# Layer 1's attention of a two-layer gated block: two items per turn, with the products of quarter size of both in one row and all others after them

## The chip, the cores and the metric

The kernel runs on one core of one Trainium2 chip. The metric is the device time of one execution in microseconds (us): the median of 13 runs. The engines are called as in the profile: PE (matrix products; PEld is its load of the stationary operand), DVE (vector), ACT (scalar functions), POOL, and SP, which issues DMAs. All five run side by side, each in its own order, and wait for each other by semaphores. All data of the stage in question are fp32, and PE takes two passes for one fp32 product, so that a product is two MATMUL records in the profile.

## The reference

Two layers, each a cross attention and a feed-forward part, both added to `x` through a gate. Batch 32, 112 rows of 256 in a batch, 375 context rows of 128. Layer 0's feed-forward is a recurrence over the batch, layer 1's a mixture of 64 experts with 8 chosen per token. What is changed is layer 1's attention:

```python
# B, N, M = 32, 112, 375; 16 heads of 64
qh = (q @ Wq).reshape(B, N, 16, 64).transpose(0, 2, 1, 3)     # q = layernorm(x), 256 wide
kh = (kv @ Wk).reshape(B, M, 16, 64).transpose(0, 2, 1, 3)    # kv = ctx, 128 wide
vh = (kv @ Wv).reshape(B, M, 16, 64).transpose(0, 2, 1, 3)
attn = softmax(einsum('bhnd,bhmd->bhnm', qh, kh) / 8)
out = einsum('bhnm,bhmd->bhnd', attn, vh).transpose(0, 2, 1, 3).reshape(B, N, 1024)
x = x + tanh(g_xattn[1]) * (out @ Wo + bo)
```

## The kernel before

The kernel has four stages in a row: layer 0's attention, the recurrence, layer 1's attention (about 810 to 1980 us of the profiled span), and the mixture of experts with its sums. Only the third is touched.

Its unit is an **item**: one batch element `b` and a group `g` of four heads, so 128 items, `n = 4b + g`. Per item these steps run; the letters are used in the rest of the text.

- **K0, K1** (`keys1`, line 796): the keys of two heads each, one product 128x128 by 375 columns; ACT copies the result to SBUF (line 800).
- **V0, V2** (`values1`, line 811): the values, two and one products of 256 columns; ACT copies the first (line 818), DVE the second (line 816).
- **S** (`scores1`, line 835): the scores of four heads, eight products of 64 rows and 64 or 48 columns of the array, four of which fit into the array at once. DVE takes the negative maximum (line 839), ACT the exponential with its sum (line 840).
- **N** (`normal1`, lines 850 and 852): DVE divides the four heads by their sums.
- **T0, T1, T2** (`turn1`, line 864): the transposes of a third of the 375 columns each, four heads in one PSUM tile; DVE copies T0 (line 871), ACT T1 and T2 (line 869).
- **A** (`values_of`, line 889): attention times values, 24 products of 64 (or 61) rows and 64 columns of the array, four at once, into two PSUM tiles, the even and the odd half of the contraction; DVE copies one and adds the other (lines 896 and 897).
- **O** (`output1`, line 907): two of the eight chunks of the output product of the batch element; after the fourth item DVE adds the bias, the gated sum and the row statistics (lines 912, 185, 156, 157), and the batch element's **route** begins.

S and A use the array in quarters of 64x64; all other products use it whole or with 112 to 128 rows. `queries1` (Q, line 783) makes one of eight chunks of the queries of two later batch elements per item, `turned1` turns the normalised rows.

`route(b)` is a generator for the choice of experts. Each `next` runs it to its next `yield`; the loop calls it twice per item, and 18 calls finish it, so that two or three are under way at any time. Three of its calls use PE: the fourth (transposes, line 225), the sixth (`pu`, lines 233 and 235) and the eighth (`pos`, lines 260 to 265). The tile `pos` is written in the eighth call and read for the last time in the ninth (line 272). The calls from the eleventh on issue one indirect DMA each from POOL (line 300).

**PSUM** has eight banks. Four are for the scores (`ps_s1`, one per head), three for everything else (`ps_m1`: K, V, T, A, Q and the route's tiles, `pos` among them), one for the output's sum (`ps_o1`), which stays open for four items. A new tile of a pool waits until an earlier one of the same pool has been read for the last time.

The order on PE, DVE and ACT is the order of the program (`manual_schedule`); POOL's isn't fixed so. Per item it is

```python
for n in range(N + 3):
    scores1(n); values_of(n - 2); output1(n - 3)
    keys1(n + 1, 0); turn1(n - 1, 0); values1(n + 1, 0, 2); turn1(n - 1, 1)
    normal1(n)                                     # then one call of each route
    keys1(n + 1, 1); turn1(n - 1, 2); values1(n + 1, 2, 1)
    # then a chunk of queries and such, and one call of each route
```

After the loop the routes that are left run to their end, then the tables of the experts' blocks are made, and the first block is loaded once they are there (line 1118).

Of the kernel before, what the change touches and what calls it, by code (L numbers as in the profile page):

```python
# [30 lines left out]
F32 = mybir.dt.float32  # L31
# [36 lines left out]
R_BO0, R_BOF, R_BO1, R_EB, R_G = 0, 256, 512, 768, 832  # L68
# [4 lines left out]
def flamingo_kernel(ctx: ExitStack, tc: tile.TileContext, a: dict, out: bass.AP):  # L73
    nc = tc.nc
# [3 lines left out]
    rtp = routes.enter_context(tc.tile_pool(name="route", bufs=1, side="right"))  # L78
# [230 lines left out]
    with ExitStack() as att:  # L309
# [14 lines left out]
        with ExitStack() as ph:  # L324
# [192 lines left out]
            def values_of(n):  # L517
                b, g = n // 4, n % 4
                pT, v = pTs.pop(n), vs[b % 2]
                del qas[n]  # L520
                if g == 0:
                    outs[b] = kvp.tile([128, 4, S], F32, tag="oU", name=f"oU_{b}")
                po = ps_m.tile([128, S], F32, tag="mm", name=f"pav0_{n}")
                for kc in range(NKC):
                    for j in range(4):
                        nc.tensor.matmul(
                            po[32 * j : 32 * j + 32, :], v[:, kc, 4 * g + j, :], pT[:, j, kc, :],
                            start=(kc == 0), stop=(kc == NKC - 1),
                        )
                nc.vector.tensor_copy(outs[b][:, g, :], po)  # L530
# [209 lines left out]
        with ExitStack() as ph:  # L740
            pp = ph.enter_context(tc.tile_pool(name="p1", bufs=2))
            kvp = ph.enter_context(tc.tile_pool(name="kv1", bufs=2))
            ps_s = ph.enter_context(tc.tile_pool(name="ps_s1", bufs=4, space=PSUM))
            ps_m = ph.enter_context(tc.tile_pool(name="ps_m1", bufs=3, space=PSUM))
            ps_o = ph.enter_context(tc.tile_pool(name="ps_o1", bufs=1, space=PSUM))
            nc.gpsimd.tensor_scalar(sdn, sdn, 0.5, None, ALU.mult)
            rstd = rstd_1
            xns, xTs, qTs, kTs, vs, ps, pTs, outs, pos = ({} for _ in range(9))
# [40 lines left out]
            def keys1(n, i):  # L789
                if n >= N:  # L790
                    return
                b, c = n // 4, n % 4 * 2 + i
                if i == 0:
                    kTs[n] = kvp.tile([128, 2, LKV], F32, tag="kT", name=f"kT1_{n}")
                pk = ps_m.tile([128, LKV], F32, tag="mm", name=f"pk1_{n}_{i}")
                nc.tensor.matmul(  # L796
                    pk, wk[:, c * 128 : (c + 1) * 128], cts[b // G][:, b % G, :],
                    start=True, stop=True,
                )
                nc.scalar.copy(kTs[n][:, i, :], pk)  # L800

            def values1(n, lo, m):
                if n >= N:
                    return
                b, g = n // 4, n % 4
                ct = cts[b // G][:, b % G, :]
                if lo == 0:
                    vs[n] = kvp.tile([KC, NKC, 256], F32, tag="v", name=f"v1_{n}", bufs=3)
                pv = ps_m.tile([KC, m, 256], F32, tag="mm", name=f"pv1_{n}_{lo}")
                for i in range(m):  # L810
                    nc.tensor.matmul(  # L811
                        pv[:, i, :], ct[:, (lo + i) * KC : (lo + i + 1) * KC],
                        wv[:, g * 256 : (g + 1) * 256], start=True, stop=True,
                    )
                if lo:
                    nc.vector.tensor_copy(vs[n][:, lo : lo + m, :], pv)
                else:
                    nc.scalar.copy(vs[n][:, lo : lo + m, :], pv)  # L818

            def scores1(n):  # L820

                if n >= N:
                    return
                b, g = n // 4, n % 4
                kT, qT, j0 = kTs[n], qTs[b // 2], b % 2 * S
                p = pp.tile([S, G, LKV], F32, tag="p", name=f"p_a1_{n}")
                nmax = small.tile([S, 4], F32, tag="nmax", name=f"nmax_a1_{n}")
                tot = small.tile([S, 4], F32, tag="tot", name=f"tot_a1_{n}")
                ps[n] = p, tot
                for j in range(4):  # L830
                    i, r0 = j // 2, 64 * (j % 2)
                    sc = ps_s.tile([S, LKV], F32, tag="s", name=f"ps_a1_{n}_{j}")

                    for q0, q1 in ((0, 64), (64, S)):
                        nc.tensor.matmul(  # L835
                            sc[q0:q1], qT[r0 : r0 + 64, 2 * g + i, j0 + q0 : j0 + q1],
                            kT[r0 : r0 + 64, i, :], start=True, stop=True,
                        )
# [60 lines left out]
            def output1(n):  # L899

                if not 0 <= n < N:
                    return
                b, g = n // 4, n % 4
                if g == 0:
                    pos[b] = ps_o.tile([S, D], F32, tag="o", name=f"po_a1_{b}")
                for c in (2 * g, 2 * g + 1):
                    nc.tensor.matmul(  # L907
                        pos[b], outs[b][:, c, :], wo[:, c, :], start=(c == 0), stop=(c == 7)
                    )
                if g == 3:  # L910
                    t = work.tile([S, D], F32, tag="t", name=f"to_a1_{b}")
                    nc.vector.tensor_tensor(t, pos.pop(b), rows[:, R_BO1 : R_BO1 + D], ALU.add)
                    gated(b, t, 1)
                    row_stats(b)
                    del outs[b]
                    routing.append(route(b, rtp, ps_m))

            ph.enter_context(tc.manual_schedule(engines={
                nc.tensor.engine, nc.vector.engine, nc.scalar.engine,
# [4 lines left out]
                turned1(0, c)  # L924
            for c in range(8):
                queries1(0, c)
            for i in range(2):
                keys1(0, i)
            values1(0, 0, 2)
            values1(0, 2, 1)  # L930
            for n in range(N + 3):
                scores1(n)
                values_of(n - 2)
                output1(n - 3)
                keys1(n + 1, 0)
                turn1(n - 1, 0)
                values1(n + 1, 0, 2)
                turn1(n - 1, 1)
                normal1(n)
                for r in routing:  # L940
                    next(r, None)
                keys1(n + 1, 1)
                turn1(n - 1, 2)
                values1(n + 1, 2, 1)

                h, c = n // 8 + 1, n % 8
                g, i = n // 16 + 1, n % 16
                if 2 <= i < 6:
                    normed1(g, i - 2)

                if 8 <= i < 12 and g + 1 < NG:
                    row_stats((g + 1) * G + i - 8)
                    if i == 11:
                        inverse_std(rstd_1, g + 1)
                if i == 8:
                    turned1(g, 1)
                if h < B // 2:
                    queries1(h, c)
                if i == 7:
                    turned1(g, 0)  # L960
                for r in routing:
                    next(r, None)
            for r in routing:
                for _ in r:
                    pass
# [429 lines left out]
```

## Time and profile before

| | us |
|---|---|
| median of 13 runs | 2550.58 (2543.97 to 2559.78) |
| the profiled execution, its own time | 2556.04 |
| its span | 2554.3 |
| mean granted PE clock | 0.958 of full |
| first S of the stage | 810.0 |
| first S of item 124 | 1937.67 |
| last S of item 127 | 1965.4 |
| start of the last `pos` product | 1992.87 |
| first block of the experts loaded (issue) | 2017.60 |

The profiled execution is 5.5 us longer than the median of the runs. Of an instruction the timeline gives the start, the duration, the engine, the line, `output<-inputs`, the active rows and columns of the array, the shape, and in brackets the idle time before it and what ended it. A line with `x16` merges sixteen instructions in a row. A duration of PE runs to the end of a matmul that is modelled, and matmuls overlap; so the text takes PE's times from start to start.

### The profile page before, as it was taken

The page shows a single profiled execution, that of the slowest core. Times are in us where ns is not written, and L with a number is a line of the kernel's source. Part 1 is how long each engine was busy: PE and PEld are TensorE (multiplying, and loading weights), DVE is VectorE, ACT ScalarE, POOL GpSimd, SP SyncE. Part 2 cuts the span into 40 slices and gives each one's busy share as a digit, 9 for nine tenths or more (in the row PEclk, how much of TensorE's full clock was granted, in tenths as well). Part 3 has the DMA queues.
Part 4 walks back from the last instruction along what each step waited for, and adds up shares of the span by engine and source line. Part 5 has one row for each costly group of instructions (what it writes and reads, how often), then busy time and mean ns, then how long its engine had stood idle before and what let it go on. Part 6 is the DMA issues. An engine that isn't in the chain of part 4 may idle for free. (4 is left out here: it accounts for less than half of the span.)

```text
span 2554.3 us, 64409 instructions
## 1 busy us (share of the span) xinstructions
PE 2310.6 (90%) x24199; PEld 1818.5 (71%) x24199; DVE 1686.4 (66%) x5065; ACT 1190.6 (47%) x3156; POOL 915.3 (36%) x1154
## 2 busy tenths in 40 slices
PE   7999999999999999999999999999999588788850
PEld 4777777779996777777777777777776366666640
DVE  5666666664327778777777877777777544455537
ACT  2555555443334555555555555555555144444430
POOL 3333333201000034333433443443334466555543
PEclk8999999999999999999999999999999698899985
DMA  3122221116300000000000000000001687567649
GB/s 84 49 57 63 59 54 49 35 32 229 110 1 1 2 26 28 28 30 28 29 29 29 29 29 29 29 29 28 30 29 33 220 275 239 157 200 224 197 130 243
DMA packets 144070, 204.54 MB, mean 80 GB/s; under 512 B 25927, under 2 KB 120729, under 8 KB 143744
## 3 DMA queue, kind: packets, MB, share of 16 engines
q1 hardware_dynamic: 100800, 99.80, 14.2%
q0 software_dynamic: 36352, 94.05, 11.4%
q10 hardware_dynamic: 6592, 6.39, 0.9%
q8 instruction: 199, 3.26, 0.6%
q14 instruction: 127, 1.04, 0.1%
HBM read 100.67 MB, written 88.74 MB: 74 GB/s over the span
## 5 line engine op out<-in xcount | busy, mean ns | idle before, releaser
L300 POOL DMA_INDIRECT xrows<-row,at x256 | 256.3, 1001 | 529.3 <-DVE at L297 339.8
L840 ACT ACTIVATE p_a<-ps_a,nmax_a 112x375 f32<-112x375 f32 x512 | 286.2, 571 | 232.2 <-DVE nmax_a L839 156.5
L486 DVE TENSOR_REDUCE nm<-sc 112x1 f32<-112x375 f32 x512 | 256.8, 543 | 183.8 <-PE st L497 136.6
L1211 POOL DMA_INDIRECT yrows<-yblk,dst x264 | 260.3, 986 | 207.6 <-ACT yblk L1199 111.0
L503 ACT ACTIVATE pT<-st 125x336 f32<-125x336 f32 x512 | 202.7, 448 | 254.1 <-PE st L497 254.1
L864 PEld LDWEIGHTS pt_a<-ident,p_a 112*125 112x125 f32 x1536 | 224.4, 188 | 78.7 <-ACT v L818 19.2
L839 DVE TENSOR_REDUCE nmax_a<-ps_a 112x1 f32<-112x375 f32 x512 | 244.4, 539 | 20.0 <-PE ps_a L835 17.1
L482 PE MATMUL sc<-kT,qp 32*112 32x375 f32 x1024 | 234.7, 528 | 3.2 <-DMA qp<-q 2.0
L497 PE MATMUL st<-qa,kT 32*125 32x112 f32 x3072 | 234.6, 284 | 0.0
L864 PE MATMUL pt_a<-ident,p_a 112*125 112x112 f32 x1536 | 228.3, 271 | 0.6 <-ACT kT L800 0.6
L811 PE MATMUL pv<-wv,c 128*125 128x256 f32 x768 | 216.4, 391 | 10.3 <-ACT kT L800 6.2
L796 PE MATMUL pk<-c,wk 128*128 128x375 f32 x512 | 208.0, 488 | 4.1
L889 PEld LDWEIGHTS pav<-pT_a,v 64*64 64x64 f32 (+1 forms) x6144 | 171.5, 133 | 45.6 <-issue 44.3
L497 PEld LDWEIGHTS st<-qa,kT 32*125 32x125 f32 x3072 | 189.0, 184 | 3.6 <-DVE nm L486 0.6
L835 PE MATMUL ps_a<-kT,qT 64*48 64x375 f32 (+1 forms) x2048 | 190.3, 486 | 0.0
L889 PE MATMUL pav<-pT_a,v 64*64 64x112 f32 (+1 forms) x6144 | 182.6, 257 | 1.9 <-issue 1.7
L852 DVE TENSOR_SCALAR p_a<-p_a,inv_a 112x375 f32<-112x375 f32 x512 | 177.7, 410 | 4.5
L800 ACT COPY kT<-pk 128x375 f32<-128x375 f32 x256 | 120.8, 472 | 106.6 <-PE pk L796 101.6
L871 DVE COPY pT_a<-pt_a 125x448 f32<-125x448 f32 x128 | 78.9, 616 | 106.0 <-PE pt_a L864 106.0
L811 PEld LDWEIGHTS pv<-wv,c 128*125 128x125 f32 x768 | 124.4, 188 | 29.4 <-ACT kT L800 21.6
L907 PE MATMUL po_a<-wo,oT 128*112 128x256 f32 x512 | 143.1, 402 | 0.0
L869 ACT COPY pT_a<-pt_a 125x448 f32<-125x448 f32 x256 | 136.6, 534 | 4.5 <-PE pt_a L864 4.1
(273 smaller groups left out, 4518.1 us busy)
## 6 DMA issues: line engine op xcount, KB each, us to landing
xblk<-xrows SPq DMA_DIRECT2D x136, 140.0 KB
xrows<-blank POOLq DMA_DIRECT2D x2, 8960.0 KB
xblk<-xrows SPq DMA_DIRECT2D x64, 280.0 KB
y<-yrows SPq DMA_DIRECT2D x32, 448.0 KB
y<-yrows SPq DMA_DIRECT2D x16, 896.0 KB
kT<-k SPq DMA_DIRECT2D x512, 23.4 KB
wall<-in_w_up SPq DMA_DIRECT2D x7, 1024.0 KB
wall<-in_w_down SPq DMA_DIRECT2D x7, 1024.0 KB
```

The source lines that it names most:

```text
L300: disjoint("xrows", nc.gpsimd.indirect_dma_start(out=xrows[:, :], out_offset=bass.IndirectOffsetOnAxis(ap=at[:, k : k + 1], axis=0), in_=r ...
L482: nc.tensor.matmul(sc, qps[b // G % 2][32 * j : 32 * j + 32, g, j0 : j0 + S], kTs[n % 6][32 * j : 32 * j + 32, :], start=True, stop=True,)
L486: nc.vector.tensor_reduce(nms[n % 3][:, j, 16:17], sc, AX.X, ALU.max, negate=True)
L497: nc.tensor.matmul(st[j][:, kc, :], kTs[m % 6][32 * j : 32 * j + 32, kc * KC : (kc + 1) * KC], qas[m][32 * j : 32 * j + 32, :], start=True ...
L503: nc.scalar.activation(pTs[m][:, j], st[j], AF.Exp)
L796: nc.tensor.matmul(pk, wk[:, c * 128 : (c + 1) * 128], cts[b // G][:, b % G, :], start=True, stop=True,)
L811: nc.tensor.matmul(pv[:, i, :], ct[:, (lo + i) * KC : (lo + i + 1) * KC], wv[:, g * 256 : (g + 1) * 256], start=True, stop=True,)
L839: nc.vector.tensor_reduce(nmax[:, j : j + 1], sc, AX.X, ALU.max, negate=True)
L840: nc.scalar.activation(p[:, j, :], sc, AF.Exp, bias=nmax[:, j : j + 1], accum_out=tot[:, j : j + 1],)
L864: nc.tensor.transpose(pt[:, j * S : (j + 1) * S], p[:, j, kc * KC : (kc + 1) * KC], ident[:S, :S],)
L889: nc.tensor.matmul(po[q][64 * r : 64 * r + 64, i, :], v[k0:k1, kc, 64 * j : 64 * j + 64], pT[k0:k1, kc, j * S : (j + 1) * S], start=(kc == ...
L1211: scatter = nc.gpsimd.indirect_dma_start(out=yrows[:, :], out_offset=bass.IndirectOffsetOnAxis(ap=dst[:, i : i + 1], axis=0), in_=y[:, i, ...
```

## The change

The loop takes two items per turn. In a row run S of `n`, A of `n - 3`, A of `n - 2` and S of `n + 1`, and then all other products of two items. The output product of a batch element is done at once, eight chunks in one go, in every second turn (where `n` is a multiple of 4), for `b = n // 4 - 2`; that of the last one comes after the last turn. The bank of `ps_o1` goes to `ps_m1`, which has four then. The normalised scores get a third buffer, the values two in place of three. The first turn's keys are made for two items ahead of the loop, and V is now made after S of its own item. Each route is still called four times per two items, and no step is left out.

```diff
-            ps_m = ph.enter_context(tc.tile_pool(name="ps_m1", bufs=3, space=PSUM))
-            ps_o = ph.enter_context(tc.tile_pool(name="ps_o1", bufs=1, space=PSUM))
+            ps_m = ph.enter_context(tc.tile_pool(name="ps_m1", bufs=4, space=PSUM))
...
-                    vs[n] = kvp.tile([KC, NKC, 256], F32, tag="v", name=f"v1_{n}", bufs=3)
+                    vs[n] = kvp.tile([KC, NKC, 256], F32, tag="v", name=f"v1_{n}")
...
-                p = pp.tile([S, G, LKV], F32, tag="p", name=f"p_a1_{n}")
+                p = pp.tile([S, G, LKV], F32, tag="p", name=f"p_a1_{n}", bufs=3)
...
+            def output1(b):
+
+                po = ps_m.tile([S, D], F32, tag="mm", name=f"po_a1_{b}")
+                for c in range(8):
                     nc.tensor.matmul(
+                        po, outs[b][:, c, :], wo[:, c, :], start=(c == 0), stop=(c == 7)
+                    )
+                t = work.tile([S, D], F32, tag="t", name=f"to_a1_{b}")
+                nc.vector.tensor_tensor(t, po, rows[:, R_BO1 : R_BO1 + D], ALU.add)
+                gated(b, t, 1)
+                row_stats(b)
+                del outs[b]
+                routing.append(route(b, rtp, ps_m))
...
+            for n in range(0, N + 4, 2):
                 scores1(n)
+                values_of(n - 3)
                 values_of(n - 2)
+                scores1(n + 1)
+                b = n // 4 - 2
+                if n % 4 == 0 and 0 <= b < B - 1:
+                    output1(b)
                 turn1(n - 1, 0)
+                values1(n - 1, 0, 2)
                 turn1(n - 1, 1)
                 normal1(n)
+                routed()
+                values1(n - 1, 2, 1)
                 turn1(n - 1, 2)
+                keys1(n + 2, 0)
+                keys1(n + 2, 1)
+                routed()
+                turn1(n, 0)
+                values1(n, 0, 2)
+                turn1(n, 1)
+                normal1(n + 1)
+                keys1(n + 3, 0)
+                turn1(n, 2)
+                routed()
+                values1(n, 2, 1)
+                keys1(n + 3, 1)
+                for n1 in (n, n + 1):
...
+                routed()
+                if n == N + 2:
+                    output1(B - 1)
```

The part left out of the last loop is the old one for `queries1`, `turned1`, `normed1` and `row_stats`, run for both items; `routed()` is one call of each route.

More of the change, by code (lines that the diff above doesn't have):

```diff
@@ L743, in flamingo_kernel @@
             ps_s = ph.enter_context(tc.tile_pool(name="ps_s1", bufs=4, space=PSUM))
-            ps_m = ph.enter_context(tc.tile_pool(name="ps_m1", bufs=3, space=PSUM))
-            ps_o = ph.enter_context(tc.tile_pool(name="ps_o1", bufs=1, space=PSUM))
+            ps_m = ph.enter_context(tc.tile_pool(name="ps_m1", bufs=4, space=PSUM))
             nc.gpsimd.tensor_scalar(sdn, sdn, 0.5, None, ALU.mult)
             rstd = rstd_1
-            xns, xTs, qTs, kTs, vs, ps, pTs, outs, pos = ({} for _ in range(9))
+            xns, xTs, qTs, kTs, vs, ps, pTs, outs = ({} for _ in range(8))
             routing = []
@@ L802, in values1 @@
             def values1(n, lo, m):
-                if n >= N:
+                if not 0 <= n < N:
                     return
@@ L897, in values_of @@
                 nc.vector.tensor_tensor(oT, po[1], oT, ALU.add)
[L899 to L906, printed above, removed]
+            def output1(b):
+                po = ps_m.tile([S, D], F32, tag="mm", name=f"po_a1_{b}")
+                for c in range(8):
                     nc.tensor.matmul(
-                        pos[b], outs[b][:, c, :], wo[:, c, :], start=(c == 0), stop=(c == 7)
+                        po, outs[b][:, c, :], wo[:, c, :], start=(c == 0), stop=(c == 7)
                     )
[L910 to L916, printed above, removed]
+                t = work.tile([S, D], F32, tag="t", name=f"to_a1_{b}")
[4 more added lines that the diff above has]
+                routing.append(route(b, rtp, ps_m))
             ph.enter_context(tc.manual_schedule(engines={
@@ L926, in flamingo_kernel, with routed @@
                 queries1(0, c)
[L927 to L931, printed above, removed]
+            for n in range(2):
+                for i in range(2):
+                    keys1(n, i)
+            def routed():
+                for r in routing:
+                    next(r, None)
+            for n in range(0, N + 4, 2):
                 scores1(n)
+                values_of(n - 3)
                 values_of(n - 2)
-                output1(n - 3)
-                keys1(n + 1, 0)
+                scores1(n + 1)
+                b = n // 4 - 2
+                if n % 4 == 0 and 0 <= b < B - 1:
+                    output1(b)
@@ L936, in flamingo_kernel @@
                 turn1(n - 1, 0)
-                values1(n + 1, 0, 2)
+                values1(n - 1, 0, 2)
                 turn1(n - 1, 1)
                 normal1(n)
-                for r in routing:
-                    next(r, None)
-                keys1(n + 1, 1)
+                routed()
+                values1(n - 1, 2, 1)
                 turn1(n - 1, 2)
[L944 to L962, printed above, removed]
+                keys1(n + 2, 0)
+                keys1(n + 2, 1)
@@ new lines, in flamingo_kernel @@
+                routed()
[9 more added lines that the diff above has]
+                for n1 in (n, n + 1):
+                    h, c = n1 // 8 + 1, n1 % 8
+                    g, i = n1 // 16 + 1, n1 % 16
+                    if 2 <= i < 6:
+                        normed1(g, i - 2)
+                    if 8 <= i < 12 and g + 1 < NG:
+                        row_stats((g + 1) * G + i - 8)
+                        if i == 11:
+                            inverse_std(rstd_1, g + 1)
+                    if i == 8:
+                        turned1(g, 1)
+                    if h < B // 2:
+                        queries1(h, c)
+                    if i == 7:
+                        turned1(g, 0)
```

## The prediction, before the change was run

> **What bounds the kernel now.** I read the page first, then the stretches, then the timeline of PE for single items.
>
> ```profile
> PE 2310.6 (90%) x24199; PEld 1818.5 (71%) x24199; DVE 1686.4 (66%) x5065; ACT 1190.6 (47%) x3156; POOL 915.3 (36%) x1154
> PE   7999999999999999999999999999999588788850
> ```
>
> The stretch from 1000 to 1400 us lies wholly in layer 1's attention (columns: length, busy us of PE, PEld, DVE, ACT, POOL, granted clock, DMA):
>
> ```profile
> 1000.00:1400.00 400.00, 392.64 (x4294) 300.77 (x4293) 313.11 (x959) 215.35 (x595) 156.64 (x203) 1.00 0.10 29
> ```
>
> PE is the bound, at full clock; DVE has 78%, so it can be late in bursts only. From 900 us on an item takes 9.17 us in the mean (116 items, S to S). An ordinary item on PE:
>
> ```profile
> 1397.53 1.49 PE L835 MATMUL ps_a<-kT,qT 64*64 64x375 f32 x16
> 1398.84 1.33 PE L889 MATMUL pav<-pT_a,v 64*64 64x112 f32 x48
> 1400.10 1.12 PE L907 MATMUL po_a<-wo,oT 128*112 128x256 f32 x4
> 1401.05 0.79 PE L796 MATMUL pk<-c,wk 128*128 128x375 f32 x2
> ...
> 1402.11 1.04 PE L811 MATMUL pv<-wv,c 128*125 128x256 f32 x4
> 1402.98 0.59 PE L864 MATMUL pt_a<-ident,p_a 112*125 112x112 f32 x4
> ...
> 1404.92 0.92 PE L783 MATMUL pq<-xTb,wq 128*128 128x224 f32 x4
> 1405.68 0.20 PE L260 MATMUL pos<-chosen,earlier 112*112 112x64 bf16 x1
> ```
>
> Starts give S 1.31, A 1.26, O 0.95, V0 0.87, Q 0.76. One item in four is slow (9.58 us), the one after `pos` was written:
>
> ```profile
> 1484.72 0.79 PE L796 MATMUL pk<-c,wk 128*128 128x375 f32 x2
> 1485.35 0.59 PE L864 MATMUL pt_a<-ident,p_a 112*125 112x112 f32 x4
> 1486.13 1.13 PE L811 MATMUL pv<-wv,c 128*125 128x256 f32 x4 [0.19 <-ACT kT L800]
> 1486.46 0.59 DVE L871 COPY pT_a<-pt_a 125x448 f32<-125x448 f32 x1
> 1487.10 0.69 PE L864 MATMUL pt_a<-ident,p_a 112*125 112x112 f32 x4
> 1488.54 0.47 DVE L272 SCALAR_TENSOR_TENSOR x<-pos,tg,x 112x256 f32<-112x256 f32 x1
> 1489.92 0.92 PE L783 MATMUL pq<-xTb,wq 128*128 128x224 f32 x4
> 1490.77 0.54 PE L835 MATMUL ps_a<-kT,qT 64*64 64x375 f32 x4
> ```
>
> V0 waits for K0's copy and T1 starts 0.05 us after T0's: each takes the bank of the tile two before it. The third bank holds `pos` until L272 has read it. The same steps at their ordinary lengths sum to 8.24, so this costs 1.34 us in each batch element.
>
> **What is removed.** (1) *Changes between quarters and the whole array.* Inside A four matmuls follow each other in 0.0955 us (single records), so twelve rounds are 1.146; A to O takes 1.26: 0.114 more. O's four of 256 columns take 0.95 where 4 x 0.2165 (V0) is 0.866: 0.088. Q before S takes 0.85 (1489.92 to 1490.77), before anything else 0.76: 0.093. S's first round of four takes 0.36 and the others 0.3145: 0.05. A pair of changes is 0.345 us. S to A is no change (0.314 as inside S), so A to S should be none. Before, rows of quarter products stand in 130 items, after in 66 turns: 64 x 0.345 = -22.1 us. PE is the bound, so all of it lies on the path, unless PE waits for something else anyway.
>
> (2) *The slow item*: its waits go with its order, about 30 x 1.34 = -40 us.
>
> O costs PE the same eight chunks. Buffers: the values of `n - 3` and `n - 2` are read before V0 of `n - 1` and `n` overwrites them, the scores' third buffer holds item `n - 1`; nothing waits there.
>
> **What is added: waits on banks and copies.** I walk a turn from its first S at 0, with DVE's maxima (0.457 from start to start, the first at 0.9, as at 1481.19 and 1482.09), A's copy and addition (0.49, 0.40), ACT's four exponentials with sums (2.33, the first 0.58 after its maximum starts: 1482.09, 1482.67), T's copies 0.54, V0's 0.59. A tile takes the bank that comes free first.
>
> (3) *The turn without O.* S, A, A, S end at 4.87, T0 V0 T1 V2 T2 run from 5.07 to 7.66 and fill the four banks. DVE: maxima to 2.73, A of `n - 3` to 3.62, A of `n - 2` (ready at 3.8) to 4.74, then the maxima of `n + 1`; ACT's exponentials of `n + 1` run from 5.32 to 7.65, and V0's copy is queued behind them: done at 8.24. K0 wants a bank at 7.66, T0's has gone to T2, so it waits 0.64, and 0.09 for a weight load that is no longer hidden: 0.73. Keys, `pu`, the second item and Q find their banks copied (DVE ends the turn with `pos`'s operations, as now). 30 x 0.73 = +22 us.
>
> (4) *The turn with O.* `pos` is written at the end of the turn before and read by L272 after N of this one, so only three banks are left while two A's want four. The second A's second tile waits for the first A's first copy: it ends at 2.73 + 0.38, plus 0.05, against 2.46: 0.70 us. S ends at 5.57, O runs from 5.77 to 9.24. DVE, done with the maxima at about 7.3, waits for O, then needs 1.55 for line 912 to line 157 (1484.92 to 1486.46) before T0's copy: 11.05 to 11.6. T0, V0, T1 end at 10.96; V2 needs V0's bank, copied by ACT at 11.38: 0.42 and 0.09. K1 waits about 0.15 to 0.25 for T2's copy or `pos`. Sum 1.45; 30 x 1.45 = +43.5. The first 0.70 is firm; the rest depends on which bank a tile is given.
>
> Behind those waits stand the same engine's copies: ACT's for K, which nobody needs before the next turn, and POOL's `rs` and row of the new route, whose transposes come 8 us later. Those cost nothing.
>
> (5) *The end.* From the first S of 124 to the last `pos` it is 55.2 us now. After, the last two O's stand behind all items, the last behind `pos` of route 30. Walked likewise: turn 124 18.0, turn 126 13.9, turn 128 up to route 30's transposes 11.6 (O, then 4.6 from line 912 to the row, as at 1982.16 to 1986.78), on to `pos` 5.1, O 3.5, then 12.4 (10.7 as now from line 912 to `pos`, 1.7 for route 30's DVE steps that now precede): 64.5. Of this 6.8 is moved there from earlier: five chunks 4.3, one A 1.15, two V 2.6, less one item's keys 1.26. So +2.5, say +3; 0 if DVE overlaps better, +10 if POOL's eight DMAs (1.25 each) precede the last `rs`.
>
> **Sum.** -22.1 - 40.2 + 21.9 + 43.5 + 3 = +6.1 us: 2556.0 becomes 2562.1 in an execution like the profiled one, which lies 5.5 above the median; on the median 2550.6 + 6.1 = 2556.7, rounded 2557.
>
> **Two rules beside this.** The Trainium skill, Perfetto Trace Analysis, Optimization Strategy, says that a gap that repeats on the busiest engine can mean too few PSUM buffers; it would promise that the fourth bank ends the bubble, and with no wait left the sum would be -59 us. TensorEngine Tiling (Array Packing), PSUM Bottleneck, speaks against the change: tiled products come faster than their results are copied out. The rows side with the second: three banks for four tiles, and copies queued behind eight maxima and eight exponentials.
>
> **The rivals.**
> - *Fewer waits than I walked* (faster): of (4) only the firm 0.70 remains, because V2, K1 find banks freed earlier. -22.1 - 40.2 + 21.9 + 21 + 3 = -16: 2534. For it: DVE is idle from 7.3 to 9.5 in that turn, and ACT from 8.3. Against it: T0's copy is fixed behind O. No wait at all would give 2491; against that stands the 0.70.
> - *DVE's order holds the second item up* (slower): banks are given in a fixed turn, T0 of item `n` needs V2's, whose copy on DVE stands behind N (1.5) and the ninth route step (1.4, 1488.54 to 1489.9). T0's copy of the first item ends at 11.6, N at 13.1, the step at 14.5, V2's copy at 14.95, while K1 ends on PE at 14.0: 0.95 more, 30 x 0.95 = +28: 2585. It decides as soon as that copy ends after 14.0.
> - *The changes cost nothing by themselves*: if the 0.345 were only the load of the first weights, which any wait hides, (1) falls away: 2579. Against it: A's last round is late before any weight of O is loaded.
> - *The order isn't what the text says*: excluded for PE, DVE and ACT, whose order is written out.
>
> **Chances.** The forecast's own case, 2550 to 2566: 0.42. Fewer waits: 0.25, none: 0.05. DVE's order: 0.18. Changes free: 0.10. The low end, 2534, is the first rival's, the high end, 2585, the second's; the rest is left out. 0.2% (5.1 us) is about what a measurement of this kernel can tell from no change. Below 2545.5: 0.30; within: 0.20, from the lower half of my own case; above 2555.7: 0.50.
>
> **What would show it.** PE at line 889: two rows of 48 in each turn, the second about 0.7 late in every second turn, with DVE's line 896 as releaser; line 796's first product 0.7 late in the turns without O, with ACT's line 818 as releaser; A to S without a gap. I am wrong if two turns with and without O sum to less than 36.0 us (now four items: 36.7), if PE waits most at line 864 of item `n`, or if the end takes over 65 us from the first S of 124.

## The result, and the profile after

The changed kernel takes 2589.34 us (median of 10 runs, 2583.41 to 2595.57) where the kernel before takes 2552.76 beside it: ratio 1.0142, 95% interval 1.0129 to 1.0156, or +36.6 us. Forecast were +6.1 and a range that ended at 2585: the sign of the likeliest case was right, the size was not. The profiled execution has a span of 2586.1 us (before: 2554.3).

The page's first engine line and its row of PE, and then the stretch from 1000 to 1400 us, answer to those shown of before:

```profile
PE 2313.1 (89%) x24199; PEld 1832.5 (71%) x24199; DVE 1714.3 (66%) x5065; ACT 1179.4 (46%) x3156; POOL 913.4 (35%) x1154
PE   7999999999989999999999999999999588888850
```
```profile
1000.00:1400.00 400.00, 380.93 (x4123) 294.57 (x4124) 311.89 (x925) 205.21 (x577) 148.31 (x194) 0.99 0.09 28
```

In the same 400 us PE did less: 380.93 us busy instead of 392.64, with 4123 products instead of 4294. PE waits more. A turn with O, from the timeline of PE and PEld:

```profile
1275.79 1.49 PE L834 MATMUL ps_a<-kT,qT 64*64 64x375 f32 x16
1277.09 1.51 PE L888 MATMUL pav<-pT_a,v 64*64 64x112 f32 x50
1278.94 1.28 PE L888 MATMUL pav<-pT_a,v 61*64 61x112 f32 x43 [0.34 <-DVE oT L895]
...
1281.51 3.71 PE L902 MATMUL po_a<-wo,oT 128*112 128x256 f32 x16
...
1287.25 0.29 PEld L810 LDWEIGHTS pv<-wv,c 128*125 128x125 f32 x2 [0.48 <-ACT v L817]
```

These are the forecast's waits, at the forecast's places. The **row** (from the first S of a turn to its first product on the whole array, here O) takes 5.72 us where a row without a wait takes 4.98 (forecast: 0.70 more, measured 0.74, releaser the first A's copy in line 895). V2 starts 0.90 us after T1 (0.425 without a wait), so it waits 0.47 (forecast 0.42). Such a turn takes 19.62 us; the prediction's steps, with the unchanged ones at their ordinary lengths, add up to about 19.5. For the turn without O they add up to about 16.7. On another chip it takes 16.48, on the chip of this profile mostly 17.5 to 17.6. What I did not see at all is one turn in eight, the one in which Q needs the newly turned x (`turned1`), and the engine that makes it late (lines chosen from the timeline of all engines):

```profile
1328.87 0.99 POOL L300 DMA_INDIRECT xrows<-row,at  x1 [0.17 <-issue]
1329.00 3.04 DVE L851 TENSOR_SCALAR p_a<-p_a,inv_a 112x375 f32<-112x375 f32 x4
1329.88 1.29 POOL L290 TENSOR_TENSOR pick<-pick,w 112x512 f32<-112x512 f32 x1
1331.96 0.67 DVE L294 TENSOR_REDUCE row<-pick 112x8 f32<-112x512 f32 x1
1333.49 0.59 DVE L773 COPY xTb<-ptx_a 128x448 f32<-128x448 f32 x1
1334.14 2.10 PE L782 MATMUL pq<-xTb,wq 128*128 128x224 f32 x6 [2.49 <-DVE xTb L773]
```

N of the second item takes 3.04 us instead of 1.39, because one of its four operations lasts 2.06 us while POOL multiplies `pick`; behind N stand `pick`'s reduction, V2's copy and the row statistics, and only then x's copy, for which PE has been waiting for 2.49 us.

The list of PE's waits from 900 to 1960 us (total, times, longest) agrees:

```profile
PE pq L782 <- DVE xTb L773: 15.5, 6, 3.0
PE pav L888 <- DVE oT L895: 9.5, 28, 0.3
PE pv L810 <- ACT v L817: 8.5, 28, 0.3
PE pav L888 <- issue: 8.2, 26, 0.3
```

The fourth line, waits inside A for which the profile names no releaser ("issue"), became the longest question of the study.

Two sums of the profile are used below: from the first S of item 0 to that of item 124, and from there to the last `pos`. Before they are 1127.7 and 55.2 us, after 1152.3 and 70.0 (forecast for the last: 64.5; over 65 was named as a sign that I am wrong). The prediction's sum puts -3.7 and +9.3 us there, since 6.8 us of work move from the loop to the end; measured are +24.6 and +14.8.

### The profile page after: what moved, and what is told of

It is laid out like the page before. It is cut to its first block, busy times and chain, and to the rows that moved or that the text cites. A ratio compares the mean times of both kernels' runs of the same rounds, so it can differ in the third digit from the quotient of the medians.

```text
span 2586.1 us, 64551 instructions
## 1 busy us (share of the span) xinstructions
PE 2313.1 (89%) x24199; PEld 1832.5 (71%) x24199; DVE 1714.3 (66%) x5065; ACT 1179.4 (46%) x3156; POOL 913.4 (35%) x1154
## 5 line engine op out<-in xcount | busy, mean ns | idle before, releaser
L851 DVE TENSOR_SCALAR p_a<-p_a,inv_a 112x375 f32<-112x375 f32 x512 | 223.0, 498 | 4.5
L888 PE MATMUL pav<-pT_a,v 64*64 64x112 f32 (+1 forms) x6144 | 188.7, 259 | 21.1 <-DVE oT L895 10.2
L834 PE MATMUL ps_a<-kT,qT 64*48 64x375 f32 (+1 forms) x2048 | 200.4, 489 | 1.1 <-ACT p_a L839 1.1
L799 ACT COPY kT<-pk 128x375 f32<-128x375 f32 x256 | 120.7, 472 | 69.9 <-PE pk L795 59.3
L817 ACT COPY v<-pv 125x512 f32<-125x512 f32 x128 | 75.2, 588 | 145.8 <-PE pv L810 135.3
L1193 DVE SCALAR_TENSOR_TENSOR h<-h,ph 128x256 f32<-128x256 f32 x132 | 55.0, 417 | 129.1 <-ACT h L1192 103.9
L210 POOL TENSOR_SCALAR rs<-stats 112x1 f32<-112x1 f32 x32 | 7.2, 225 | 376.6 <-DVE stats L157 374.3
```

Of the source, the lines that this page charges most:

```text
L851: nc.vector.tensor_scalar(p[:, j, :], p[:, j, :], inv[:, j : j + 1], None, ALU.mult)
L888: nc.tensor.matmul(po[q][64 * r : 64 * r + 64, i, :], v[k0:k1, kc, 64 * j : 64 * j + 64], pT[k0:k1, kc, j * S : (j + 1) * S], start=(kc == ...
```

## The experiments

Ratios are to the kernel before, on the same chip; differences to the changed kernel are those of the ratios. The runs fell on several chips. On the one of the profiles above, here called the first, the kernel before takes 2550 to 2554 us; on the others 2438 or 2439. Of this difference most lies behind layer 1's attention, but not all, as will be seen.

### One suspect at a time: a1, a2, a3 and b1, on the first chip

a1 moves one instruction of the route, from its ninth call to its eighth:

```diff
         nc.vector.tensor_tensor(slot, pr, e_row, ALU.add)
+        nc.vector.scalar_tensor_tensor(xb, po[:, :D], tg[:, 3:4], xb, ALU.mult, ALU.add)
         ...
-        nc.vector.scalar_tensor_tensor(xb, po[:, :D], tg[:, 3:4], xb, ALU.mult, ALU.add)
```

> The changed kernel, with the addition of `pos` to x (L272) moved from the ninth to the eighth call of the route, so that the bank of `pos` comes free about 6 us earlier, before the next turn with O begins. Bank theory: the second A of the turn with O no longer waits for the first A's copy, the row S, A, A, S falls from 5.72 to 5.0, and K1's 0.15 of waiting goes too: 30 x 0.75 to 0.9 = 22 to 27 us less than the changed kernel, ratio to the kernel before 1.004 to 1.006. Rival, DVE's lateness: the wait is for DVE itself, which now has 0.47 us more to do just before the maxima of the next turn; then the row stays at 5.7 and the time does not move (1.014), or the second A waits elsewhere.

Measured: 1.0013 (1.0001 to 1.0026), 33 us less than the changed kernel (31 by the medians), more than forecast. In the turns with O the row falls to 4.98, V2's wait goes as well (T1 to V2 0.425 instead of 0.893), the first two K take 1.28 instead of 1.52: 18.20 us instead of 19.62. The bank of `pos` was the cause of nearly all of term (4), V2's wait included, which I had put down to V0's copy alone. The rival was half right too, on this chip: the rows of the turns without O became 0.28 longer in the mean, and there V2's copy ends 0.91 us after the row's first S instead of 0.52, behind the moved instruction of 0.47.

a2 puts both halves of `turned1` behind the queries of the turn before:

```diff
-                    if i == 8:
-                        turned1(g, 1)
                     ...
                     if i == 7:
                         turned1(g, 0)
+                        turned1(g, 1)
```

> The changed kernel, with both halves of turned1 at the end of the turn without O (items n%16 == 7), behind that turn's queries; so that no queries wait in the turn with O for x's copy, which stands behind the late normalisation. Theory A (x's copy is late because DVE is late): the eight turns in which Q takes 4.3 to 5.9 us instead of 1.5 fall to 1.5, 7 x 2.8 = 13 to 20 us less, ratio 1.006 to 1.009. Rival (DVE is late whatever stands there, and Q's banks wait for DVE's copies anyway): Q stays above 3 us in these turns and the ratio stays 1.014.

Measured: 1.0069 (1.0047 to 1.0090), 19 us less. Q takes 1.51 in all turns. Theory A holds: these waits were x's copy and nothing else.

a3 gives the scatters to other calls (the routes of the last two batch elements stay as they were):

```diff
+        if not late:
+            yield
+            yield
         for k in range(TOPK):
             ...
-            if not late or k % 2:
+            for _ in range((k % 2) if late else (0, 1, 1, 2, 0, 1, 0, 0)[k]):
                 yield
```

> The changed kernel, with the eight scatters of a route given to other calls: none in the last two calls of a turn with O, none in the last call of a turn without O, so that POOL issues none while PE runs S, A, A, S. Theory B (two scatters issued back to back by POOL hold up PE's instructions in the first A): the row of the turns without O falls from 5.7-6.2 to 5.0, 28 x 0.9 = 25 us less, ratio 1.003 to 1.006. Rival (the row waits for something on DVE or for a bank, and the scatters only stand beside it): the row stays at 5.7 to 6.2 and the ratio is 1.012 to 1.016.

Measured: 1.0280 (1.0261 to 1.0298), 35 us more than the changed kernel, outside both expectations. Most rows of the turns without O rose to 6.5 to 7.5 although no scatter stood beside them. DVE's list of waits shows why, first a3's line, then the changed kernel's:

```profile
DVE row L294 <- POOL pick L290: 82.9, 26, 3.5
```
```profile
DVE row L294 <- POOL pick L290: 2.6, 1, 2.6
```

Two scatters of 1 us each now stood ahead of `pick` on POOL, DVE waited 3.2 us for it in every batch, and V2's copy, for which the first A waits, ended 2.3 to 2.6 us after the row's first S instead of 0.5. POOL is 35% busy and off the path by its share; by its place it isn't.

b1 prices the changes between quarters and the whole array, by one more pair per item in the kernel before:

```diff
                 scores1(n)
-                values_of(n - 2)
                 output1(n - 3)
+                values_of(n - 2)
```

> The kernel before, with the output chunk of item n-3 put between the scores of item n and the values of item n-2. Each item then changes between quarter and whole-array products twice instead of once, nothing else is added. Theory C (a pair of changes costs 0.345 us of PE's time by itself): 128 x 0.345 = +44 us, ratio 1.017. Rival (the changes cost nothing that a wait would not hide): +0 to +11 us (only a weight load of 0.09 that is no longer hidden), ratio 1.000 to 1.004.

Measured: 1.0202 (1.0180 to 1.0225), +52 us. The sum over the items alone rose by 48.0, 0.387 per item. An item of b1 on PE, from O to T0:

```profile
1399.70 1.12 PE L907 MATMUL po_a<-wo,oT 128*112 128x256 f32 x4
1400.75 1.38 PE L889 MATMUL pav<-pT_a,v 64*64 64x112 f32 x48
1402.06 0.90 PE L796 MATMUL pk<-c,wk 128*128 128x375 f32 x2
1402.80 0.59 PE L864 MATMUL pt_a<-ident,p_a 112*125 112x112 f32 x4
```

Without any wait, S, O, A and K0 take 0.35 us more than S, A, O and K0 before: S 1.415 instead of 1.31, O 1.047 instead of 0.954, A 1.31 instead of 1.26, and K0, which now stands behind A, 0.735 instead of 0.63. The items that wait for nothing else show the same sum (8.95 became 9.31). The slow item rose by 0.86, by waits for copies. So the changes are not free, and the 0.345 of term (1) was right.

### The copies behind N: a4, a5, and three edits together: a6; on a second chip

In the turns without O the first A's two tiles take the banks of V2 and of the first Q, the second A's first tile that of the second Q; all three copies are DVE's and end 0.52, 0.82 and 1.12 us after the row's first S in the profile after. On the first chip such rows took 6.2 us, and 4.99 to 5.05 where the copies had ended by 0.37 and PE ran at full clock (items 14, 42 and 90; four others with copies as early stand behind a turn in which PE waited for x, began slowly and took 5.4 to 6.6). So a4 gives the copies to ACT:

```diff
-                if lo:
+                if lo and n % 2:
                     nc.vector.tensor_copy(vs[n][:, lo : lo + m, :], pv)
 ...
-                nc.vector.tensor_scalar(qTs[h][:, c, :], pq, 0.125, None, ALU.mult)
+                nc.scalar.activation(qTs[h][:, c, :], pq, AF.Copy, scale=0.125)
```

> The changed kernel, with V2's copy of item n (the last V2 of a turn) and the copies of the queries on ACT instead of DVE. Theory D (the row of the turn without O is held up by DVE's copies of V2 and Q, which the first and second A wait for, and which stand behind DVE's late normalisation of item n+1): the row falls from 5.7-6.2 to 5.0, 28 x 0.75 to 1.2 = 21 to 33 us less than the changed kernel, ratio 1.002 to 1.006; the turn with O keeps its 0.74 (the bank of `pos`). Rival (the row is held up by PE's own instruction stream, whatever frees the banks): the row stays at 5.7 to 6.2, ratio 1.014. A third: ACT's copies delay its first exponential, and the row gains but T0 and K0 lose as much.

Measured: 1.0097 (1.0077 to 1.0117); rows of 4.98 in all ordinary turns. It looked like theory D, with less gain than expected. The runs d1 and d3 below showed that it was not.

a5 multiplies `pick` on DVE:

```diff
-        side.tensor_tensor(
+        nc.vector.tensor_tensor(
             pick, pick, w.unsqueeze(1).to_broadcast([S, TOPK, E]), ALU.mult
         )
```

> The changed kernel, with the multiplication of `pick` (L290) on DVE instead of POOL. Theory E (DVE's normalisation of item n+1 in the turn with O takes 3.1 us instead of 1.4 because POOL multiplies `pick` beside it): with the multiplication on DVE the four L851 take about 1.4 to 2.0 us, DVE itself has 0.7 to 1.3 us more, and ends the turn 0.4 to 1 us earlier; rows without O at 5.0 to 5.7, ratio 1.004 to 1.010. Rival (the stretch comes from the scatter that POOL issues there): L851 stays at 3.1 us, DVE ends the turn 0.7 to 1.3 later, ratio 1.015 to 1.025.

Measured: 1.0069 (1.0050 to 1.0088). The group of the normalisation from 1000 to 1800 us, in the kernel before, after, and in a5 (busy us, mean ns of one):

```profile
L852 DVE TENSOR_SCALAR p_a<-p_a,inv_a 112x375 f32<-112x375 f32 x346 | 120.1, 410 | 3.1
```
```profile
L851 DVE TENSOR_SCALAR p_a<-p_a,inv_a 112x375 f32<-112x375 f32 x334 | 149.0, 508 | 2.9
```
```profile
L851 DVE TENSOR_SCALAR p_a<-p_a,inv_a 112x375 f32<-112x375 f32 x342 | 118.7, 410 | 3.0
```

Theory E holds: it is the multiplication on POOL, not the scatter, which still runs beside N in a5 (23 normalisations beside a scatter, 0.41 us each). `pick` takes 0.69 on DVE instead of 1.28 on POOL. But N's stretch is only a part of what makes x late: the turns in which Q waits for x take 21.7 to 23.5 us in a5, 24.2 to 24.7 in d1 (the changed kernel on the fifth chip, below), where the other turns of this kind take 19.62 or 19.63 in both.

a6 has the edits of a1, a2 and a4 at once.

> The changed kernel with three edits at once: `pos` added to x in the eighth call, both halves of turned1 at the end of the turn without O, V2's copy of item n and the copies of the queries on ACT. If the three causes are separate and cover the loss (bank of `pos`, x behind DVE, V2 and Q behind DVE), both rows take 5.0, no Q over 1.6, and the turns fall to about 18.1 and 16.8: 34.9 for four items where the kernel before takes 36.7, ratio 0.978 to 0.988. Rival (DVE's or ACT's lateness only moves on): 1.000 to 1.005.

Measured: 0.9855 (0.9833 to 0.9876). The turns take 18.20 and 16.48, Q 1.51; the list of PE's waits has one line left, the forecast's K0:

```profile
PE pk L794 <- ACT v L816: 6.4, 27, 0.2
```

b2 is the kernel before with a1's edit alone.

> The kernel before, with `pos` added to x in the eighth call of the route, so that its bank comes free before the item that was slow. My term (2): the slow item's 1.34 goes without any other change, 30 x 1.34 = -40 us, ratio 0.984. Rival (DVE's 0.47 ahead of the maxima delays A's copies instead): 0.995 to 1.000.

Measured: 0.9853 (0.9833 to 0.9873), as good as a6. Its item takes 8.82 us in the mean from item 32 to 112, and the slow item 8.36 instead of 9.58. This is term (2) by itself, and it came without the change.

### The end: a7 and a8, on a third chip

In a6 the loop to item 124 takes 1067.5 us, in b2 1082.1; from there to the last `pos` it is 66.2 against 51.6. The pairing wins 14.6 and gives 14.5 back. a7 is a6 with O a turn earlier, a8 adds a5's edit:

```diff
-                b = n // 4 - 2
-                if n % 4 == 0 and 0 <= b < B - 1:
+                b = (n - 6) // 4
+                if n % 4 == 2 and 0 <= b < B - 1:
                     output1(b)
```

> The kernel with all three edits (a6), and with each batch's output a turn earlier: in the turn n%4 == 2, right behind the row that ends its last A, instead of in the turn n%4 == 0 after it. If the end costs what I read in the profiles (from the first S of 124 to the last `pos` 66.2 us in a6 against 51.6 in the kernel before with `pos` early, 6.8 of it moved work), O and route of batch 30 begin 16 to 18 us earlier and the end shortens by 4 to 10 us: ratio to the kernel before 0.981 to 0.984. Rival: O now waits for the oT of the row just ahead of it, or x's transposes and the route's steps meet in another turn, and each turn loses 0.2 to 0.5 us: 0.985 to 0.995.

> The kernel a7 with the multiplication of `pick` on DVE as well. If POOL's multiplication still stretches a normalisation on the path, 28 x 0.1 to 0.3 = 3 to 8 us less than a7; if not, DVE's added 0.7 us costs 0 to 5 us. Either way the four L851 take about 410 ns each.

Measured: a7 0.9853 (0.9835 to 0.9870), the end at 66.3: the earlier O did not shorten it, and my reading of the end failed. a8 0.9845 (0.9831 to 0.9859), the lowest ratio of the study, not separable from a7 or b2; no normalisation is stretched in it (0.45 us at most).

### What holds PE up inside A: c1 to c4, d1 to d4

On the first chip the rows were long although the copies ended before the products were due (1.31 and 2.46 us after the first S). c1 and c2 leave DVE as it is in a4 and only let the banks come free later, by repeating one copy on ACT:

```diff
-                nc.scalar.copy(kTs[n][:, i, :], pk)
+                for _ in range(4 if n % 4 == 3 and i else 1):    # c2: 5
+                    nc.scalar.copy(kTs[n][:, i, :], pk)
```

> The kernel a4 (V2 and Q copied by ACT, DVE as late as in the changed kernel), with K1's copy of the turn with O made four times over on ACT, which leaves DVE and POOL alone and only lets the banks of the next row come free later: by ACT's lengths (0.47 a copy) the first A's two tiles at about 0.3 and 0.65 us after the row's first S, the second A's at 1.0 and 1.35, all before those products are due (1.31 and 2.46). Theory F (a wait at which PE's instruction stream stands costs time though it ends before the product is due, because PE has then no instructions in hand): rows without O longer than 4.98, 5.3 to 6.2, 28 x 0.3 to 1.2 = 9 to 34 us more than a4. Rival (a wait that ends before the product is due costs nothing, and the row was held up by something else on DVE): rows stay at 4.98, ratio as a4, 1.010.

> As c1, with K1's copy made five times over: the first A's tiles free at about 0.75 and 1.1, the second A's at 1.5 and 1.8, still before they are due. Theory F: rows without O of 5.7 to 6.4, 0.3 or more longer than in c1. Rival: 4.98 to 5.1.

Measured, on the first chip: 1.0125 (1.0088 to 1.0163) and 1.0148 (1.0101 to 1.0196). Most rows take 6.14 to 6.29 in c1, where the copies ended at 0.38, 0.64 and 0.89; in c2 6.22 to 6.28, hardly longer. This fits theory F in kind, but not by dose, and a4 itself, with the banks free early, was not run on this chip.

c3 and c4 were meant to leave the scatters out of a part of the loop, in c1 and in the changed kernel:

```diff
+            if b in range(10, 17):
+                put.append((row, at[:, k : k + 1]))   # scattered behind the last item
+                yield
+                continue
             disjoint("xrows", nc.gpsimd.indirect_dma_start(
```

> The kernel c1, with the 56 scatters of the routes of batches 10 to 16 kept back until behind the last item; for the steady loop that leaves six pairs of turns in which POOL issues no scatter and their transfers are absent, beside the others in the same run; the whole takes longer for the scatters at its end, which says nothing. Theory F alone (a wait ahead of the product costs PE its instructions in hand): rows without O of 6.1 to 6.3 in these turns too. Theory F with B (only both together hold PE up: no instructions in hand, and scatters that slow the supply of the next): rows of 5.0 to 5.4 in these turns, 6.1 to 6.3 in the others.

> The changed kernel, with the 56 scatters of the routes of batches 10 to 16 kept back in the same way. Theory F alone: rows without O of 5.7 to 6.2 in these turns as in the others (V2's copy still ends at 0.5, unless DVE is earlier without POOL's scatters). F with B: 5.0 to 5.4. L851 of item n+1 stays near 3.1 us per four, since `pick` is still multiplied on POOL beside it, or falls below 2 if the scatter was the cause.

Both failed as tests: POOL's order isn't written out, and it issued the kept scatters inside the loop; besides, the edit dropped the `yield` behind the scatters of the other routes, so that all eight of such a route came one after the other. But they fell on a fourth chip (one run each, 2453.79 and 2469.38 us where the kernel before took 2437.55), and there rows took 4.98 with c1's waits, with scatters at the same places and with scatters one behind the other. So chip and edit were mixed up, and the last four runs repeat the changed kernel, the kernel before, a4 and c1 on one chip, a fifth.

> The changed kernel unaltered, once more, beside the kernel before, a4 and c1 on one chip. On the chip of the record rows without O took 5.7 to 6.2, ratio 1.014. If those rows are a matter of V2's and Q's copies alone, they take the same here whatever the chip. If they are a matter of the chip (its supply of instructions to PE), then on a chip where the kernel before takes 2438 us they take 5.0 to 5.5, and the ratio is 1.006 to 1.012; where it takes 2550, again 1.014.

> The kernel before unaltered, for its profile on the same chip: an item of 9.17 us from 900 us on if chips do not differ here; 9.05 to 9.1 if the hold-ups in its first A (11.5 us in all) are the chip's too.

> The kernel a4 once more, beside the changed kernel on one chip. If V2's and Q's copies hold the row up: rows without O of 4.98 on any chip, 20 to 30 us less than the changed kernel where that one's rows take 5.7 to 6.2. If the rows are the chip's: the same row lengths as the changed kernel on this chip.

> The kernel c1 once more, beside a4 on one chip. If an early wait costs by itself, rows without O of 6.1 to 6.3 again, on any chip. If only a chip on which the kernel before takes 2550 us shows it: there 6.1 to 6.3, elsewhere 4.98.

Measured: the changed kernel 1.0138 (1.0117 to 1.0159), a4 1.0107 (1.0090 to 1.0125), c1 1.0092 (1.0075 to 1.0109). The same row of the same program, with the same three copies ending at 0.52, 0.82 and 1.12, on PE's timeline, first on the first chip, then in d1:

```profile
1258.20 1.49 PE L834 MATMUL ps_a<-kT,qT 64*64 64x375 f32 x16
1259.51 1.66 PE L888 MATMUL pav<-pT_a,v 64*64 64x112 f32 x38
1261.49 1.62 PE L888 MATMUL pav<-pT_a,v 61*64 61x112 f32 x57 [0.33 <-issue]
```
```profile
1251.31 1.49 PE L834 MATMUL ps_a<-kT,qT 64*64 64x375 f32 x16
1252.61 2.48 PE L888 MATMUL pav<-pT_a,v 64*64 64x112 f32 x96
1254.91 1.45 PE L834 MATMUL ps_a<-kT,qT 64*48 64x375 f32 x16
```

6.18 us to T0 on the first chip, 4.99 on the fifth; c1's rows take 4.98 there too. Theory D falls on this chip: a4 gains nothing in the ordinary rows; what it gains over the changed kernel (5.9 us of medians, the intervals overlap) lies in the turns next to `turned1`. Theory F falls here too (d4's rows are a4's); on the first chip the rows agree with it, but nothing there separates it from other causes. The kernel before shows the same difference: its A loses about 11 us over the loop on the first chip and none in d2, whose item takes 9.13 us where the profile of the record had 9.21 (items 32 to 112). So the hold-ups slow both kernels. The loop loses 24.6 us by the change on the first chip and 18.4 on the fifth, the end 14.8 and 17.9, and the ratio comes out nearly the same.

## Why the prediction was wrong, point by point

Per batch element, from item 32 to 112, the change costs 1.05 us on the fifth chip (36.50 to 37.55) and 1.24 on the first (36.85 to 38.08). The steps of the prediction, in us per batch element:

| step | forecast | measured | from |
|---|---|---|---|
| (1) two pairs of changes less | -0.69 | -0.71 | b1 |
| (2) the slow item | -1.34 | -1.21 | b2 against d2, on the second and the fifth chip |
| (3) turn without O: K0 | +0.73 | +0.47 | T2 to K 0.82 instead of 0.425; first two K 1.36 instead of 1.29 |
| (4) turn with O | +1.45 | +1.53 | row 0.74, V2 0.47 and 0.09, K 0.23 |
| Q behind x's copy | none | +0.67 | d1: 24.2 us over 27 batch elements, less 6.0 before |
| rows after normed1 and turned1 | none | +0.21 | d1: 6.0 us over 29 |

The measured lines sum to 0.96, the forecast's to 0.15. So the walk was right in its ordinary turns (19.62 and 16.48 in d1 against about 19.5 and 16.7), and the A to S passage without a change was right (row 4.98). Of its four terms (3) was off most, by 0.26; and (4) charged V2's wait to V0's copy, where a1 shows the bank of `pos` behind it.

**The step that failed** is that nothing was charged for Q. (4) stops at K1, and (3) says: "Keys, `pu`, the second item and Q find their banks copied (DVE ends the turn with `pos`'s operations, as now)". DVE ends the turn late, and in one turn in eight Q waits not for a bank but for the copy of the new x. I walked DVE up to T0's copy and took the rest over from before, where N did not stand beside POOL's multiplication. Moved beside it, N takes 3.04 us instead of 1.39, and x's copy stands behind it. This wait, with the reduced clock that follows it, costs 0.67 us per batch element more than before; moving x's copy alone took it away (a2: Q 1.51 in all turns, 19 us). I had a rival for a late DVE, but put it at V2's bank in the turn with O and priced it at +28; the place was wrong, and that the size came out near is luck.

On the first chip the distribution differs: rows of the turns without O +1.0, Q behind x +0.5, less 0.4 that the kernel before loses in its own rows; with the first four lines this gives 1.2. There long rows go with late copies of V2 and Q; on the fifth chip the same late copies cost nothing in the ordinary rows. What holds PE up on the first chip stays open.

(5), the end, was walked as 64.5 and is 70.0 (69.9 in d1). Of the surplus, 2.1 stands in turn 126 (16.0 instead of 13.9; its row takes 7.05) and 3.4 behind the transposes of route 30 (24.4 instead of 21.0); in d1 it is 0.8 and 4.8. Why an earlier O (a7) gave nothing back stays open; the routes that are left are drained one after the other, which I did not vary.

Together: by the profiles, the loop costs 28.3 us more than the sum had put there on the first chip (24.6 against -3.7) and 22.1 on the fifth, the end 5.5 and 8.6 (+14.8 and +17.9 against +9.3). By the medians 30.5 and 27 us are missing; what lies ahead of and behind these stretches is 7.6 us shorter in the profile after on the first chip and 1.9 longer on the fifth. So about five sixths of the miss on the first chip are the loop's, and the rest is the end's. The rival "fewer waits" fell: every wait of (4) came. The rival "changes cost nothing" fell by b1.

The two rules of the Trainium skill that I had set beside the sum: TensorEngine Tiling (Array Packing), PSUM Bottleneck, agrees with K0's wait for V0's copy (0.47 us of a turn without O); the larger waits of the turn with O do not show it, since they were one bank that `pos` held (a1: 1.42 us). Perfetto Trace Analysis, Optimization Strategy, was borne out in its way: the repeating gap of the kernel before was a bank, but what freed it was reading `pos` earlier (b2: -1.5%), not another bank beside a new order.

## What to carry to other kernels

When a bank is short, ask first who holds it longest, and move that reader: one instruction moved by one call was worth 1.5%, as much as the new order with three repairs. When an order is changed, walk every engine to the end of the period, POOL's two-input operations included, and look at which of them now run beside which DVE operation; then check the rare turns (here one in eight) by themselves. And compare variants on one chip before a cause is named: a4 looked like a cure, and the rows that it seemed to cure are as short without it on a chip as fast. When the price of one step is read from starts, go on to the product behind it: b1's K0 held 0.105 of the 0.35 us.

## What the runs showed of the hardware

- **DVE beside POOL.** One normalisation of 0.41 us lasted 2.06 us beside POOL's two-input multiplication of 1.29 us; it ended 0.2 us after it, in all 20 cases from 1000 to 1800 us. Beside POOL's operation on the route's row, with one large input (1.77 us, at 1250.87 in the profile after), two normalisations took 0.41 each. The Trainium skill, SBUF — State Buffer, Who interferes with whom, says that DVE and GpSimd share one pair of ports as an exclusive lock (DVE for some of its operations), and that the one that comes second waits in full. That DVE was held until POOL was done agrees with this; the order does not, since by the profile the normalisation had started 0.55 us ahead of the multiplication, and that nothing was lost beside the row operation does not follow from it alone.
- **Half a clock after a wait.** In the turn shown above PE waited 2.49 us for x. The granted clock (last column but two) in the stretches after it, on the profile after:

```profile
1334.00:1336.50 2.50, 2.36 (x8) 1.88 (x8) 1.22 (x5) 0.00 (x0) 0.00 (x0) 0.64 0.16 50
1336.50:1338.50 2.00, 2.00 (x17) 0.97 (x20) 0.62 (x3) 0.35 (x1) 0.94 (x1) 0.60 0.00 0
1338.50:1341.00 2.50, 2.50 (x104) 2.39 (x100) 2.28 (x6) 2.32 (x8) 0.00 (x0) 1.00 0.18 57
```

  S's first two rounds of four take 0.66 and 0.63 us there instead of 0.36 and 0.31. The turn takes 23.65 us instead of 19.62, 0.4 of it `turned1`'s own work, and the row behind it 5.74 instead of 4.98: a wait of 2.5 us so costs about 4 us, and that is part of the 0.67 above. In d1 the clock in the 3 us behind the wait for x is 0.55.
- **Rows of quarter products stall on one chip.** With the same program and copies that end at the same times, rows of quarter products, whose instructions follow each other every 12 ns (four loads and four products in 0.0955 us), stalled by 1.2 us on one chip and not at all on another. What PE lacks there was not found. The transfers in the queue of instructions are as long as on the others (median 1.1 us), and they do not go with the stalls: of 34 gaps of over 0.3 us inside A in the profile after (rows without O, leaving out those that begin at the reduced clock), 10 overlap such a transfer.
- **The last stage is where the chips differ most**: from the last `pos` to the end the kernel before takes 561 us on the first chip and 455 in d2, with the DMA engines 71% and 84% busy.
